# Other places for the mask preparation in the emission order of a two-layer graph network kernel

## Chip, cores and metric

The kernel runs on one core of one Trainium2 chip. The metric is the device time of one execution in microseconds (us); the median of three runs of the kernel before is 3479.84 us (3477.9 to 3487.6).

## The reference

Sixteen graphs of 1024 nodes with 256 features each go through two layers, each added to its input. `adj` is an int32 matrix of 1024 x 1024 zeros and ones per graph.

```python
h = relu(layernorm(x))                              # layer 0: masked attention + MLP
n = layer_norm(h, gamma1, beta1)                    # query = key = value = n, 8 heads of 32
scores = einsum('bhqd,bhkd->bhqk', n, n) / sqrt(32)
attn = softmax(where(adj[:, None] > 0, scores, -inf))
h = h + einsum('bhqk,bhkd->bhqd', attn, n)
x = x + h + gelu(layer_norm(h, gamma2, beta2) @ W1 + b1) @ W2 + b2
f = relu(layernorm(x))                              # layer 1: graph attention
g = f @ W
e = leaky_relu(g @ a_1 + (g @ a_2).T + (g @ a_12) @ g.T, 0.2)
p = softmax(where(adj > 0, e, -9e15))
x = x + elu(f @ W_1 + (p @ f) @ W_2)
```

Both layers use the same adjacency.

## The kernel before, in words

All work on one graph is a batch `b`. The attention of layer 0 for batch `b` (`attention`, L954) is done at the same time as the MLP and layer 1 of batch `b - 1` (`rest`, L1099), so that TensorE always has something to do.

**Units and groups.** The attention of a batch is cut into 32 units (qh, g, kt): half of the queries (512), group of four heads, tile of 128 keys. A unit scores its keys against its queries (L975, 16 small matmuls into two PSUM tiles `s`), adds the mask (L996, VectorE, two instructions of 128 x 1024) and takes the exponential (L999, ScalarE) into an SBUF tile `e`. In the next unit TensorE multiplies `e` with the values (L1012). A group is the eight units with the same half and the same heads; it ends after units 8, 16, 24 and 32. The sums of the exponentials over the keys are made by DMA: GpSimd issues for each `e` an accumulating DMA into the group's first tile (L1036, 512 KB each). The pool of `e` has five buffers; a buffer comes free when its accumulating DMA has landed. Two to three units after the end of a group TensorE adds up the accumulated tiles over the partitions (`den`, L914), which waits for the last accumulations.

In batch 0 there is no `rest` beside the attention. There half of the mask additions are done by TensorE, with a matmul of the mask and an identity (L968), and half of the sums by VectorE (L1023).

**Masks.** For each half of the queries, four tiles of 128 rows of the adjacency are prepared (`turn_masks`, L875):

- `fetch_mask` (L579): two DMAs of 256 KB each (128 x 512 int32) on SP's queue, L583. The pool has two such buffers, so a tile can be fetched only once the one before it is converted.
- `convert_mask` (L587): two VectorE instructions (L591) turn 0 and 1 into a large negative number and 0 in fp8, tile `mq` (two buffers).
- a transposing DMA on SP's queue (L887) puts the tile into `mk`, the mask of that half of the queries with the keys on partitions.

The generator makes one step at a time: step 0 fetches tile 0; step 1 converts tile 0 and fetches tile 1; step 2 transposes tile 0, converts tile 1 and fetches tile 2; step 3 and 4 go on in the same way; step 5 transposes tile 3. A mask `mk` lives for two batches, since layer 1 of the same graph reads it one batch later (L1266). The pool `mkp` has four: those of two batches. Step 2 is the first to write into the buffer of the same half of two batches before. The first half of batch 0 is prepared in `prologue` (L822 to L854) and isn't touched by the change.

**Order.** Every engine works its instructions in the order in which they are emitted, kept by L1495 to L1504. The order is made by streams, generators that say at which place they want to go on (L1474 to L1479): the stream with the smallest place makes its next step. Places are counted in batches. `stream_a` puts attention unit k of batch b at place b + k/32. `stream_b` puts the pieces of `rest` beside them, by their estimated TensorE time against 134 us per batch. `stream_c` puts the loading and normalizing of the next batch (`prologue`, L760) at b - 0.70 to b - 0.25. `stream_m` (L1461) puts the steps of the masks; `spread` (L1409) divides the stretch from start to end into five, and step i is made at start + i/5 of it. Small deferred pieces are inserted by an estimated clock (`defer`, L743).

Of the kernel before, what the change touches and what calls it, by code (L numbers as in the profile page):

```python
# [493 lines left out]
def fast_path(  # L494
# [84 lines left out]
    def fetch_mask(b, t):  # L579
        halves = []  # L580
        for c in range(0, N, QW):
            a = adjp.tile([P, QW], I32, tag="adj", name=f"adj_{b}_{t}_{c}")
            nc.sync.dma_start(a, rows(adj, b, t, slice(c, c + QW)))  # L583
            halves.append(a)
        return b, t, halves

    def convert_mask(b, t, halves):  # L587

        m = mqp.tile([P, N], FP8, tag="mq", name=f"mq_{b}_{t}")
        for i, a in enumerate(halves):  # L590
            nc.vector.tensor_scalar(  # L591
                m[:, i * QW : (i + 1) * QW], a, 0.0, NEG8, op0=ALU.is_le, op1=ALU.mult, saturate=False
            )
        return m
# [280 lines left out]
    def turn_masks(b, qh, st):  # L875

        ts = list(range(qh * TPH, (qh + 1) * TPH))
        raw = fetch_mask(b, ts[0])
        yield
        m = mkp.tile([P, NT // 2, QW, 2], FP8, tag="mk", name=f"mk_{b}_{qh}")  # L880
        st[qh] = m
        pairs = m.rearrange("p m q r -> p m (q r)").bitcast(BF16)
        mq = convert_mask(*raw)
        raw = fetch_mask(b, ts[1])
        for i in range(TPH):
            yield
            nc.sync.dma_start_transpose(pairs[:, :, i * P : (i + 1) * P], mq.bitcast(BF16))  # L887
            if i + 1 < TPH:
                mq = convert_mask(*raw)
            if i + 2 < TPH:  # L890
                raw = fetch_mask(b, ts[i + 2])
# [517 lines left out]
    def spread(pieces, n, start, end):  # L1409
        yield start  # L1410
        for i, _ in enumerate(pieces):
            yield start + (end - start) * (i + 1) / n

    states = [{} for _ in range(B + 1)]
# [46 lines left out]
    def stream_m():  # L1461
        for b in range(B):
            for qh in range(b == 0, NQH):
                yield from spread(turn_masks(b, qh, states[b]), 5, b + 0.5 * qh - 0.27, b + 0.5 * qh - 0.07)

    def stream_s():
        yield -0.3
# [3 lines left out]
        for i, _ in enumerate(check_products()):  # L1471
            yield 1.32 + 0.04 * i

    streams = [stream_s(), stream_a(), stream_b(), stream_p(), stream_c(), stream_m()]  # L1474
    places = [next(s, None) for s in streams]
    while any(p is not None for p in places):
# [93 lines left out]
```

## Time and profile before

| | |
|---|---|
| median of 3 runs | 3479.84 us |
| all runs | 3477.9, 3479.84, 3487.6 us |
| the profiled execution, its time | 3473.44 us |
| the profiled execution, its span | 3471.6 us, mean granted TensorE clock 0.997 |
| VectorE waits for an adjacency fetch (L591), whole span | 14.0 us in 14 waits, longest 4.1 us |
| PE waits for the mask addition (L975 for L996), whole span | 3.1 us in 2 waits |
| adjacency fetch, from issue to landing | min 3.0, median 5.6, max 10.6 us |
| transposing DMA, from issue to landing | median 6.2 us |
| conversion (L591), one instruction | median 0.42 us |
| DMA engines, share of the span by queue | GpSimd's (accumulations) 71.3%, SP's 15.5% |

How to read it: a stretch of the trace is given as from:to in us from the start of the span. "Busy" is the time in which an engine executes; the DMA share is the mean busy share of the core's 16 DMA engines, and goes over 1 where times of packets overlap. An arrow in brackets behind a line tells how long the engine was idle before it, and what ended that. The first attention unit starts at 25.6 us; those of batch 0 take 126 us in all, those of batch 1 207 us, later ones 211 to 212 us. In batch 4, unit 0 starts at 782.6 us.

### The profile page before, as it was taken

The numbers are of one execution on the slowest core, as the hardware profiler recorded it, in microseconds if no ns is written. First come the engines' busy times: TensorE is split into PE (matmuls) and PEld (weight loads), VectorE is DVE, ScalarE is ACT, GpSimd is POOL, SyncE is SP. The second block draws the span as 40 slices with busy tenths as digits, with TensorE's granted clock in tenths as the row PEclk, the third lists the DMA queues.
The fourth block names the chain that finished last, engine by engine and source line by source line (L and its number), as shares of the span: only waits on it lengthen the run. The fifth ranks groups of instructions, "written<-read, shape, count | busy, mean of one in ns | idle before, by whom it ended". The sixth has DMA issues, their size and how long they took to land.

```text
span 3471.6 us, 119040 instructions
## 1 busy us (share of the span) xinstructions
PE 3424.4 (99%) x52478; PEld 1648.9 (47%) x52478; DVE 2749.4 (79%) x5194; ACT 1857.3 (53%) x2184; POOL 1418.5 (41%) x1708
## 2 busy tenths in 40 slices
PE   6999999999999999999999999999999999999998
PEld 2244444444444444444444444444444444444477
DVE  6788788787888878888788887878888788887754
ACT  5555555555555555555555555555555555555522
POOL 4443443434434344443444434344343444434220
PEclk9999999999999999999999999999999999999999
DMA  8798989899899998989999899998999989899720
GB/s 193 147 186 171 187 163 191 177 188 192 161 190 177 187 192 165 185 171 190 189 167 188 170 187 182 183 188 167 189 177 193 187 164 185 166 192 182 152 62 14
DMA packets 281906, 598.56 MB, mean 172 GB/s; under 512 B 94882, under 2 KB 130084, under 8 KB 281380
## 3 DMA queue, kind: packets, MB, share of 16 engines
q0 software_dynamic: 124416, 453.04, 71.3%
q1 hardware_dynamic: 156676, 137.56, 15.5%
q8 instruction: 414, 6.78, 0.8%
q14 instruction: 112, 0.92, 0.1%
q10 hardware_dynamic: 288, 0.26, 0.0%
HBM read 104.21 MB, written 16.78 MB: 35 GB/s over the span
## 4 chain that ended last, share of the span: by engine, by line
PE 95%; DMA 2%; DVE 1%; issue 1%; ACT 1%; POOL 0%; SPq 0%; POOLq 0%; DVEq 0%; ACTq 0%
PE s L975 15%; PE o L1012 14%; PE pa L570 12%; PE ph L570 12%; PE lg L570 12%; PE po L570 11%; PE pf L570 3%; PE pg L570 3%; PE puT L570 3%; PE den L914 2%; DMA acc<-e 2%; PE pty L1142 1%; PE ptos L946 1%; PE ptk L808 1%; PE ptf L1218 1%; PE pa L567 1%
## 5 line engine op out<-in xcount | busy, mean ns | idle before, releaser
L999 ACT ACTIVATE e<-e 128x1024 f32<-128x1024 f32 x852 | 895.9, 1057 | 947.0 <-DVE e L996 703.3
L1036 POOL DMA_DIRECT2D acc<-e x864 | 757.3, 892 | 1444.9 <-DMA acc<-e 657.8
L996 DVE TENSOR_TENSOR e<-s,mk 128x1024 f32<-128x1024 f32 x852 | 1003.2, 1217 | 185.4 <-PE s L975 151.4
L975 PE MATMUL s<-kT 32*64 32x512 f32 x8192 | 578.3, 616 | 3.1 <-DVE odd L996 3.1
L1012 PE MATMUL o<-e,va 128*32 128x512 f32 x3456 | 463.8, 606 | 2.1 <-ACT e L999 2.1
L570 PE MATMUL pa<-gw,e 128*32 128x258 f32 x7648 | 455.2, 380 | 0.0
L570 PE MATMUL lg<-fT,uT 128*32 128x256 f32 x7680 | 449.3, 379 | 0.0
L570 PE MATMUL ph<-yT,w 128*32 128x256 f32 x7808 | 447.8, 379 | 0.0
L570 PE MATMUL po<-w,hid 128*32 128x256 f32 x7680 | 439.8, 379 | 0.0
L570 PEld LDWEIGHTS ph<-yT,w 128*32 128x32 f32 x7808 | 259.4, 110 | 197.8 <-issue 42.5
L570 PEld LDWEIGHTS po<-w,hid 128*32 128x32 f32 x7680 | 249.9, 110 | 209.4 <-issue 62.2
L570 PEld LDWEIGHTS lg<-fT,uT 128*32 128x32 f32 x7680 | 259.1, 110 | 189.3 <-issue 38.5
L570 PEld LDWEIGHTS pa<-gw,e 128*32 128x32 f32 x7648 | 253.4, 110 | 198.7 <-issue 48.8
L1272 ACT ACTIVATE e<-e,shift 128x512 f32<-128x512 f32 x256 | 183.1, 717 | 187.2 <-DVE e L1271 167.0
L1266 DVE SCALAR_TENSOR_TENSOR e<-lg,gw,mk 128x256 f32<-128x256 f32 x512 | 223.0, 477 | 71.1 <-PE lg L570 60.7
L1169 DVE TENSOR_TENSOR hid<-ph,b1c 128x512 f32<-128x512 f32 x256 | 175.2, 687 | 86.0 <-PE ph L570 74.6
L1012 PEld LDWEIGHTS o<-e,va 128*32 128x32 f32 x3456 | 69.0, 108 | 354.9 <-issue 226.6
L1271 DVE SCALAR_TENSOR_TENSOR e<-e 128x512 f32<-128x512 f32 x256 | 196.2, 766 | 8.8
L999 ACT ACTIVATE acc<-acc 128x1024 f32<-128x1024 f32 x124 | 130.9, 1057 | 130.2 <-DVE acc L996 125.8
L975 PEld LDWEIGHTS s<-kT 32*64 32x64 f32 x8192 | 121.1, 130 | 163.8 <-issue 108.4
L996 DVE TENSOR_TENSOR acc<-s,mk 128x1024 f32<-128x1024 f32 x124 | 146.0, 1217 | 20.6 <-PE s L975 20.5
L800 POOL TENSOR_TENSOR nrm<-nrm,g 128x256 f32<-128x256 f32 x128 | 113.1, 884 | 61.7 <-DVE nrm L734 61.7
(146 smaller groups left out, 3820.1 us busy)
## 6 DMA issues: line engine op xcount, KB each, us to landing
acc<-e POOLq DMA_DIRECT2D x864, 512.0 KB, 6.2
adj<-in_adj_dram SPq DMA_DIRECT2D x248, 256.0 KB, 5.5
h<-in_x_dram SPq DMA_DIRECT2D x64, 256.0 KB, 6.0
xb<-in_x_dram SPq DMA_DIRECT2D x128, 128.0 KB, 4.6
out_dram<-z SPq DMA_DIRECT2D x128, 128.0 KB, 3.7
adj<-in_adj_dram SPq DMA_DIRECT2D x4, 512.0 KB, 6.9
mk<-mq SPq DMA_TRANSPOSE x128, 6.2
w<-in_L_gnn_W_dram SPq DMA_DIRECT2D x2, 1024.0 KB
```

Source lines behind the costliest of these rows:

```text
L570: nc.tensor.matmul(out[c : c + HD], lhsT[:, c : c + HD], rhs, start=start, stop=stop)
L800: nc.gpsimd.tensor_mul(nrm, nrm, g1)
L914: nc.tensor.matmul(den[j * HD : (j + 1) * HD, :], ones, acc[j // 2][:, j % 2, :], start=acc is accs[0], stop=acc is accs[-1],)
L975: nc.tensor.matmul(sc[j // 2][c : c + P // 2, j % 2, :], kT[r, g, kt * P + c : kt * P + c + P // 2], kT[r, g, qs], start=j >= by_pe, stop= ...
L996: nc.vector.tensor_tensor(e, masked, mb, op=ALU.add)
L999: weights = lambda e=e, masked=masked: nc.scalar.activation(e, masked, AF.Exp, scale=SCALE)
L1012: nc.tensor.matmul(o[j * HD : (j + 1) * HD, :], va[:, kt, (g * GH + j) * HD : (g * GH + j + 1) * HD], es[j // 2][:, j % 2, :], start=(kt = ...
L1036: nc.gpsimd.dma_start(sums[g, qh][i], e, accum_op=ALU.add)
L1169: nc.vector.tensor_tensor(hid[:, f0 : f0 + 2, :], ph, b1c[:, f0 : f0 + 2].unsqueeze(2).to_broadcast([P, 2, CW]), op=ALU.add,)
L1266: nc.vector.scalar_tensor_tensor(e[:, j, :], lg[:, j, :], gw[:, kt, D : D + 1], st[c // 2][:, kt // 2, qs, kt % 2], op0=ALU.add, op1=ALU.add,)
L1271: nc.vector.scalar_tensor_tensor(e, e, ALPHA, e, op0=ALU.mult, op1=ALU.max)
L1272: ready = defer(2.5, lambda: nc.scalar.activation(e, e, AF.Exp, bias=shift))
```

## The change

One line: the places between which the five steps of a mask are spread. Stretches in batches, b being the batch that the mask is for.

```diff
     def stream_m():
         for b in range(B):
             for qh in range(b == 0, NQH):
-                yield from spread(turn_masks(b, qh, states[b]), 5, b + 0.5 * qh - 0.27, b + 0.5 * qh - 0.07)
+                yield from spread(turn_masks(b, qh, states[b]), 5, b + (-0.34, 0.05)[qh], b + (-0.10, 0.40)[qh])
```

| in units of the batch in which it is made | start, end before | distance of steps | start, end after | distance of steps |
|---|---|---|---|---|
| first half (made in the batch before) | 23.4, 29.8 | 1.28 | 21.1, 28.8 | 1.54 |
| second half (made in the same batch) | 7.4, 13.8 | 1.28 | 1.6, 12.8 | 2.24 |

The second half is first read in unit 16, the first half in unit 0 of its batch. The number and kind of instructions on every engine and queue stay as they are.

## The prediction, made blind

> **What bounds the kernel now.** I read the page's busy table and its chain first, then the chain in order of time, then the busy time by stretches of one batch, then the start-up. From the page:
>
> ```profile
> PE 3424.4 (99%) x52478; PEld 1648.9 (47%) x52478; DVE 2749.4 (79%) x5194; ACT 1857.3 (53%) x2184; POOL 1418.5 (41%) x1708
> ...
> PE   6999999999999999999999999999999999999998
> ...
> PE 95%; DMA 2%; DVE 1%; issue 1%; ACT 1%; POOL 0%; SPq 0%; POOLq 0%; DVEq 0%; ACTq 0%
> ```
>
> TensorE has work from the second fortieth of the span to the last and carries 95% of the chain. Busy time alone doesn't say that there is no stall inside it, so I look at the rhythm. The chain in order of time shows the same stage (the logits matmuls, L570) once per batch:
>
> ```profile
> 540.59 3.52 PE lg L570 x64
> ...
> 752.51 3.52 PE lg L570 x64
> ...
> 963.36 3.52 PE lg L570 x64
> ...
> 1174.19 3.52 PE lg L570 x64
> ...
> 3074.81 3.52 PE lg L570 x64
> ```
>
> The distances are 211.92, 210.85 and 210.83 us. The shortest returns in many batches, so I take 210.84 us as the period without a stall. From the first to the last of these lines are 12 batches in 2534.22 us, or 211.19 each: over 12 batches all stalls together are 12 x 0.35 = 4.2 us, over the 14 steady batches 4.9 us. No change of places alone can win more there.
>
> Busy time by stretches of batch 4 (units 0 to 4, 4 to 9, 9 to 14, 14 to 21, 21 to 25, 25 to 30, 30 to 32; columns: length, busy us of PE, PEld, DVE, ACT, POOL, clock, DMA share, GB/s):
>
> ```profile
> 782.60:809.10 26.50, 26.50 (x432) 12.05 (x432) 19.14 (x30) 15.77 (x17) 11.11 (x14) 1.00 0.78 156
> 809.10:843.70 34.60, 34.60 (x566) 16.79 (x560) 26.98 (x50) 19.25 (x16) 15.55 (x20) 1.00 0.95 189
> 843.70:877.90 34.20, 34.20 (x571) 16.86 (x567) 27.92 (x63) 19.19 (x22) 15.06 (x19) 1.00 1.05 218
> 877.90:922.00 44.10, 44.10 (x656) 19.73 (x656) 34.47 (x69) 24.00 (x35) 22.61 (x28) 1.00 0.76 143
> 922.00:950.60 28.60, 28.60 (x456) 13.34 (x444) 25.63 (x43) 15.55 (x22) 11.46 (x14) 1.00 0.88 175
> 950.60:979.90 29.30, 29.30 (x504) 14.52 (x496) 25.38 (x54) 14.52 (x19) 9.72 (x11) 1.00 1.10 210
> 979.90:993.50 13.60, 13.60 (x225) 6.45 (x217) 12.89 (x24) 7.67 (x10) 5.32 (x6) 1.00 1.02 208
> ```
>
> The two stretches in which masks are made now (843.7 and 950.6) have the fullest DMA, 1.05 and 1.10; the others have 0.76 to 1.02. VectorE is fullest at the end (12.89 of 13.60). PE is full in all of them: the crowding costs it nothing in this batch.
>
> In the start-up there are real gaps:
>
> ```profile
> 60.00:80.00 20.00, 18.06 (x292) 6.80 (x285) 14.80 (x35) 11.61 (x19) 6.07 (x8) 0.99 0.95 203
> 80.00:100.00 20.00, 17.78 (x184) 4.37 (x183) 17.09 (x34) 12.97 (x17) 13.17 (x16) 0.84 0.59 117
> ...
> 120.00:140.00 20.00, 17.48 (x192) 4.90 (x186) 10.47 (x18) 8.64 (x9) 3.79 (x4) 0.91 0.78 161
> 140.00:160.00 20.00, 18.12 (x230) 6.70 (x232) 18.69 (x27) 7.23 (x7) 7.21 (x9) 0.91 0.96 213
> ```
>
> and in order of time, two of them begin with a mask conversion that waits for its adjacency:
>
> ```profile
> 74.59 0.90 DVE L591 TENSOR_SCALAR mq<-adj 128x512 fp8e5<-128x512 int32 x2 [0.98 <-DMA adj<-in_adj_dram]
> ...
> 77.95 1.09 PE L975 MATMUL s<-kT 32*64 32x512 f32 x8 [1.27 <-DVE odd L996]
> ...
> 140.01 0.43 DVE L591 TENSOR_SCALAR mq<-adj 128x512 fp8e5<-128x512 int32 x1 [1.15 <-DMA adj<-in_adj_dram]
> ...
> 142.91 1.09 PE L975 MATMUL s<-kT 32*64 32x512 f32 x8 [1.88 <-DVE odd L996]
> ```
>
> VectorE waits 0.98 and 1.15 us, the masked addition behind it (L996) is late, and PE waits 1.27 and 1.88 us for it. A third (4.12 us at 127) coincides with a wait of PE for the last accumulating DMA (2.35 us). After the first and the third the granted clock of the stretch drops: 20 x 0.16 = 3.2 us and twice 20 x 0.09 = 1.8 us, 6.8 us in all.
>
> **What the skill says.** "Perfetto Trace Analysis", section "Identifying the Most-Contended Engine": matmul busy time is no good measure of the distance from the limit. That is why I use the period; the trace agrees in so far as batches with 99 to 100% busy time differ by 1.1 us. "DMA: Bandwidth & Descriptors", section "Issuing engines are not separate DMA queues": DMAs of all issuing engines run on the same 16 engines and interleave. The shares above 1 where masks and accumulations meet agree. "TensorE: Matmul & The Clock Gate", section "Part 1": the array falls to half clock after an idle window of about 3.4 us. Here the clock fell after gaps of 1.3 to 2.4 us, shorter than that, so I count the clock as something that may or may not be lost with each gap.
>
> **The change, part by part.** Nothing is added or removed: the same 124 mask tiles (31 half-batches of four), each of two fetches of 256 KB, two conversions and one transposing DMA, are put elsewhere. With 32 attention units per batch, the old places of the four transposes are units 9.9, 11.2, 12.5, 13.8 (second half) and 25.9, 27.2, 28.5, 29.8 (first half of the next batch); the new ones 6.1, 8.3, 10.6, 12.8 and 24.2, 25.7, 27.3, 28.8. The distance from a fetch to its conversion grows from 1.28 units to 2.24 and 1.54.
>
> 1. *Conversions on VectorE.* Two of 0.42 us per tile, in order with everything else. The built order shows them ahead of L996 of units 4, 7, 9 and 11 (before: 9, 10, 12, 13) and 23, 25, 26 and 28 (before: 25, 26, 28, 29). Behind a moved conversion wait L996, ScalarE's exponential and then PE. By the instructions in order of time (end of L996, start of the next unit's L975; smallest of batches 3 to 14), L996 ends 3.7, 3.5, 1.7 and 2.8 us ahead of the next unit's scores in units 4, 7, 9, 11, and 4.1, 2.0, 2.6 and 0.5 in 23, 25, 26, 28. The last carries a conversion already, so 0.84 us is covered everywhere; without that cover it would cost up to 0.84 us a batch. Unit 29, also with 0.5 us to spare, loses its conversion. Some of the small steady stalls lie there: I take 1 us over all batches, bounds 0 and 2.4.
>
> 2. *Fetches and transposes on the DMA engines.* SP's hardware queue moved 137.56 MB in 15.5% of 3471.6 us, 3.9 us per MB of all engines' time: 2.0 us for a tile's fetch; for its transpose of 0.13 MB in small packets at least 0.5, and I take 0.8. Counted by the new places, units 9 to 14 (843.7) lose two fetches and a transpose, 4.8 us of 34.2: 1.05 to 0.91. Units 0 to 4 gain two fetches, 4.0 of 26.5: 0.78 to 0.93. Units 4 to 9 gain a transpose: 0.95 to 0.97. Units 25 to 30 give one fetch to units 21 to 25: 1.10 to 1.03, and 0.88 to 0.95. The crests fall. What a crest cost: accumulations late, their e buffers late, L996 waiting, 6.9 us in eight waits from 220 to 3300 us, of which PE sees at most the 4.9 us. I take 1.5 us saved, bounds -2.5 and +14 (rival B).
>
> 3. *SP's queue.* The first transpose writes the buffer that the masks of two batches ago held; its last reader is now just ahead. In the built order the output store ahead of it on SP waits for a later VectorE instruction than that reader, so the wait is covered and costs nothing. Behind it on SP stand the next fetches, wanted 1.5 units (some 10 us) later against 5.6 us to landing: covered too. Loads of x (L770) are passed by one or two fetches; nobody waits for them at once. POOL's queue holds no step of the change; its accumulations only share the engines.
>
> 4. *Start-up.* Units of batch 0 last some 2.8 to 4 us, so 1.28 units are 4 to 5 us, less than the 5.6 us median to landing: hence the waits. 2.24 units are about 6.5 us, 1.54 about 4.5. The second half of batch 0 should lose its wait (1.27 us of PE, and the clock's 3.2 if it follows the gap); batch 1's first half stays short of the landing. The first tile comes behind the weights on SP's queue, whose transfers ended near 39 us; its conversion is due near 40 us: no stall, at most 1 us. Saved: between -2 and 12 us; I take 2.5.
>
> **Sum.** 1 + 1.5 + 2.5 = 5 us. The profiled execution took 3473.44 us (span 3471.6 and 1.8 around it): 3468.4 after. The median of the runs is 6.4 us above it, 3479.84: forecast 3475.
>
> **Rivals.** (A) *Nothing moves*: PE is the bound and only other covered work shifts. For it: PE is full in all seven stretches; against: the start-up gaps. 3480 to 3484. (B) *Slower*: short crests. In units 6 and 8 a fetch and a transpose now start together, 2.8 us of DMA work in some 6 us whose share was 0.91 to 0.98 already. Accumulations finish up to 2.8 us later, an e buffer comes late, L996 waits, and beyond the 2.0 us that it has to spare in unit 6 PE stops. With accumulations late by their usual jitter too (longest wait for one 1.7 us) I price it at 1.0 us in each of 14 batches: +14 us, 3494; it is slower beyond the bound from 0.75 us per batch. For it: only 5 e buffers. Against: averages of 1.05 and 1.10 over five units are borne now. (C) *Everything comes back*: 4.9 steady, the two waits of 1.27 and 1.88, and 6.8 of clock, less a little: about -15 us, 3465.
>
> **Numbers.** Forecast 0.52 (3470 to 3480), A 0.18, B 0.14, C 0.16. A measurement of this kernel tells about 0.3% (10.4 us) from no change: faster 0.16, same 0.70, slower 0.14. The range 3462 to 3489 leaves out B and the far third of C, 0.19.
>
> **What would show it.** Right: period 210.84 with fewer longer batches; no wait of L591 near 60 and 75 us; DMA share near 0.91 in units 9 to 14; PE still 99%. Wrong: a period that exceeds 210.84 in every batch, waits of L996 for accumulations in units 4 to 9, or a new wait of L591 near 40 us.

## The result and the profile after

The changed kernel takes 3535.1 us (median of 4 runs, 3522.24 to 3545.12); the kernel before, in runs beside it, 3483.72 us (4 runs, 3477.9 to 3496.59). The ratio is 1.0150, 95% interval 1.0127 to 1.0173: slower by some 51 us. That is far above the range. The profiled execution of the changed kernel took 3545.12 us (span 3543.3, mean clock 0.994), the slowest of the four; its span is 71.7 us longer than that of before.

The page after, in the parts that the prediction read first:

```profile
PE 3451.1 (97%) x52478; PEld 1669.8 (47%) x52478; DVE 2757.9 (78%) x5194; ACT 1857.6 (52%) x2184; POOL 1415.8 (40%) x1708
...
PE 82%; DMA 11%; DVE 4%; issue 2%; ACT 1%; POOL 0%; SPq 0%; POOLq 0%; DVEq 0%; ACTq 0%
```

PE has fallen from 99% to 97%, and DMA from 2% to 11% of the chain: transfers now release the work that ends last. Which ones, the two lists of waits say (line waited for: us in total, times, longest). PE's first:

```profile
PE den L914 <- DMA acc<-e: 38.9, 14, 7.1
```

and VectorE's:

```profile
DVE mq L591 <- DMA adj<-in_adj_dram: 38.0, 33, 3.8
...
DVE e L996 <- DMA acc<-e: 8.8, 6, 2.2
```

The same two lines in the kernel before:

```profile
PE den L914 <- DMA acc<-e: 2.3, 1, 2.3
...
DVE mq L591 <- DMA adj<-in_adj_dram: 14.0, 14, 4.1
```

So there are two new waits, and neither is the one that the prediction feared: L996 waiting for an `e` buffer stands at 8.8 us, of 6.9 before.

Where in a batch they lie shows when the start of every attention unit (first L975 matmul of a unit) is listed and the shortest length of each unit over batches 2 to 14 is subtracted. The shortest lengths add up to 210.81 us per batch in both kernels. In batches 2 to 15 of the changed kernel unit 10 is too long by 49.6 us in all (0 to 10.8 a batch; before 1.0), units 26 to 30 by 14.1 us (before 3.2). Batch 1 is 11.4 us longer than before. These are 48.6 + 10.9 + 11.4 = 70.9 of the 71.7 us. The start-up saved nothing: batch 0 lasts 125.8 us in both.

Not all of the 49.6 us is standing still. `den` waits 29.3 us of it; and behind the waits of four batches the granted clock is at half for 3 to 6 us of work, 18.1 us in all, so that some 9 us are lost there (an estimate from the clock records). Behind the wait of batch 6, for instance (the 0.50 is the clock):

```profile
1304.60:1311.40 6.80, 4.36 (x40) 1.82 (x44) 0.00 (x0) 1.54 (x2) 0.00 (x0) 0.50 0.93 208
```

The rest of the 49.6 us was not followed.

**Unit 10.** The chain in order of time, changed kernel, batch 6, the end of the first group:

```profile
1277.54 7.77 DMA acc<-e
...
1285.84 6.12 DMA acc<-e
...
1292.50 14.49 DMA acc<-e
1306.99 0.04 issue
1307.04 0.65 PE den L914
```

and the timeline of the same stretch:

```profile
1279.63 4.21 SPq L887 DMA_TRANSPOSE mk<-mq  x1
...
1285.84 0.85 POOL L1036 DMA_DIRECT2D acc<-e  x1 [4.08 <-DMA acc<-e]
...
1291.33 2.61 SPq L887 DMA_TRANSPOSE mk<-mq  x1
...
1292.50 0.85 POOL L1036 DMA_DIRECT2D acc<-e  x1 [1.62 <-DMA acc<-e]
...
1293.99 5.76 SPq L770 DMA_DIRECT2D h<-in_x_dram  x2
...
1307.04 1.07 PE L914 MATMUL den<-acc,ones 128*32 128x512 f32 x2 [6.98 <-DMA acc<-e]
```

An accumulating DMA adds into the tile that an earlier one wrote, so its issue on POOL waits for that one to land (the 4.08 us in brackets). A group has two tiles and so two such chains; the three accumulations above are of one. One that is stretched by a transpose beside it puts all later ones of its chain back. The last one, issued 0.9 us after unit 9 began, meets a transpose, two loads of x and the first two accumulations of the next group, and takes 14.5 us; PE stands still for 6.98 us. In the same batch before, the last one was issued 1.0 us ahead of unit 9 and landed 1.0 us after unit 10 began:

```profile
1261.51 0.85 POOL L1036 DMA_DIRECT2D acc<-e  x1 [1.61 <-ACT acc L999]
```

Over batches 2 to 14 the last accumulation of the first group landed on average 0.9 us ahead of the start of unit 10 before, at the latest 2.8 us after it; the matmuls of `den` that read it begin 2.4 us after that start when nothing holds them up. In the changed kernel it landed 4.6 us after it on average, at the latest 10.0. The last accumulations of the second and third group hardly differ (within 0.6 us on average).

The places are not yet the times of issue: SP issued the transposes ahead of them. By the traces (median of batches 2 to 14) the second half's four are issued at 5.0, 7.2, 9.1 and 11.0 units in the changed kernel, at 9.2, 10.4, 12.0 and 12.7 before. `den` begins near 10.2. So three are ahead of it where there was one, and the new ones are those at 5.0 and 7.2.

**Unit 26.** The timeline of the changed kernel, batch 4, units 25 to 27:

```profile
964.90 0.75 DVE L591 TENSOR_SCALAR mq<-adj 128x512 fp8e5<-128x512 int32 x2
965.02 0.34 SPq L1318 DMA_DIRECT2D out_dram<-z  x1
...
965.41 2.03 SPq L887 DMA_TRANSPOSE mk<-mq  x1
...
967.54 1.00 SPq L583 DMA_DIRECT2D adj<-in_adj_dram  x2
...
973.77 0.43 DVE L591 TENSOR_SCALAR mq<-adj 128x512 fp8e5<-128x512 int32 x1 [2.44 <-DMA adj<-in_adj_dram]
...
975.43 0.43 DVE L591 TENSOR_SCALAR mq<-adj 128x512 fp8e5<-128x512 int32 x1 [1.24 <-DMA adj<-in_adj_dram]
...
976.79 3.69 PE L570 MATMUL pa<-gw,e 128*32 128x258 f32 x64 [0.98 <-DVE e L1266]
...
977.29 2.35 DVE L996 TENSOR_TENSOR e<-s,mk 128x1024 f32<-128x1024 f32 x2
```

The tile is converted at 964.90, its buffers come free, but the next fetch stands on SP behind an output store and the transpose of the tile before, and is issued at 967.54. Its conversion comes one unit later and waits 2.44 and 1.24 us. The work behind it on VectorE (L1266 of layer 1, then L996) is late, and PE with it. The conversions in units 25 and 26 waited 29.8 us in batches 2 to 14, of 0.9 before.

**What the prediction had named as signs.** Busy time by stretches of batch 4, changed kernel, same units as before:

```profile
800.10:826.60 26.50, 26.50 (x432) 12.03 (x432) 18.19 (x30) 15.79 (x17) 9.81 (x14) 1.00 0.81 167
826.60:861.20 34.60, 34.60 (x564) 16.83 (x560) 28.24 (x52) 19.29 (x16) 16.11 (x20) 1.00 1.02 207
861.20:896.20 35.00, 35.00 (x572) 17.98 (x565) 28.15 (x59) 19.34 (x22) 15.91 (x20) 1.00 0.95 194
```

The crest in units 9 to 14 fell as said, from 1.05 to 0.95 (0.91 forecast), and units 4 to 9 rose from 0.95 to 1.02 (0.97 forecast); units 0 to 4 stand at 0.81 (0.93 forecast). The shares look harmless, with no stretch above the crest of before; yet it is in the third of these stretches that the stalls of most batches lie.

### The profile page after: what moved, and what is told of

It reads as the page before. It is cut to its first block, busy times and chain, and to the rows that moved or that the text cites. A ratio compares the mean times of both kernels' runs of the same rounds, so it can differ in the third digit from the quotient of the medians.

```text
span 3543.3 us, 119080 instructions
## 1 busy us (share of the span) xinstructions
PE 3451.1 (97%) x52478; PEld 1669.8 (47%) x52478; DVE 2757.9 (78%) x5194; ACT 1857.6 (52%) x2184; POOL 1415.8 (40%) x1708
## 4 chain that ended last, share of the span: by engine, by line
PE 82%; DMA 11%; DVE 4%; issue 2%; ACT 1%; POOL 0%; SPq 0%; POOLq 0%; DVEq 0%; ACTq 0%
PE s L975 13%; PE pa L570 11%; PE o L1012 11%; PE lg L570 11%; DMA acc<-e 9%; PE po L570 9%; PE ph L570 8%; PE pg L570 3%; PE puT L570 3%; PE pf L570 3%; PE den L914 1%; DMA adj<-in_adj_dram 1%; DVE e L996 1%; PE ptf L1218 1%; PE ptk L808 1%
## 5 line engine op out<-in xcount | busy, mean ns | idle before, releaser
L996 DVE TENSOR_TENSOR e<-s,mk 128x1024 f32<-128x1024 f32 x852 | 1003.2, 1217 | 201.1 <-PE s L975 140.7
L975 PE MATMUL s<-kT 32*64 32x512 f32 x8192 | 582.5, 614 | 1.5 <-DVE e L996 1.5
L570 PE MATMUL ph<-yT,w 128*32 128x256 f32 x7808 | 459.4, 380 | 0.0
L570 PE MATMUL po<-w,hid 128*32 128x256 f32 x7680 | 457.3, 383 | 0.0
L570 PEld LDWEIGHTS lg<-fT,uT 128*32 128x32 f32 x7680 | 261.7, 110 | 186.9 <-issue 38.9
L1266 DVE SCALAR_TENSOR_TENSOR e<-lg,gw,mk 128x256 f32<-128x256 f32 x512 | 222.9, 476 | 53.9 <-PE lg L570 43.8
L975 PEld LDWEIGHTS s<-kT 32*64 32x64 f32 x8192 | 122.4, 130 | 164.6 <-issue 97.9
L996 DVE TENSOR_TENSOR acc<-s,mk 128x1024 f32<-128x1024 f32 x124 | 146.1, 1218 | 20.6 <-PE s L975 20.4
L1196 DVE TENSOR_TENSOR xb<-po,xb 128x256 f32<-128x256 f32 x128 | 54.3, 424 | 130.6 <-PE po L570 115.4
```

The source lines that it names most:

```text
L570: nc.tensor.matmul(out[c : c + HD], lhsT[:, c : c + HD], rhs, start=start, stop=stop)
L975: nc.tensor.matmul(sc[j // 2][c : c + P // 2, j % 2, :], kT[r, g, kt * P + c : kt * P + c + P // 2], kT[r, g, qs], start=j >= by_pe, stop= ...
L996: nc.vector.tensor_tensor(e, masked, mb, op=ALU.add)
L1196: nc.vector.tensor_add(xt[t], po, xt[t])
L1266: nc.vector.scalar_tensor_tensor(e[:, j, :], lg[:, j, :], gw[:, kt, D : D + 1], st[c // 2][:, kt // 2, qs, kt % 2], op0=ALU.add, op1=ALU.add,)
```

## The experiments

All ratios are to the kernel before, run beside them on the same chip. The diffs are shortened, and shown against the changed kernel; those of experiments 9 and 10 against the kernel before.

**1 and 2. Each half alone.**

```diff
-  b + (-0.34, 0.05)[qh], b + (-0.10, 0.40)[qh]
+  b + (-0.34, 0.23)[qh], b + (-0.10, 0.43)[qh]      # first half only
+  b + (-0.27, 0.05)[qh], b + (-0.07, 0.40)[qh]      # second half only
```

> Only the first half of the queries has the new places (start -0.34, end -0.10); the second half has the old ones. Theory (accumulations of the group that ends after unit 8 land late because mask DMAs run beside them in units 4 to 10, and TensorE waits for them at den, L914): the long stall at unit 10 goes, the small one at unit 26 stays (about 10 us over the run in the trace of after), so 3485 to 3497. Rival (VectorE: conversions and their waits for adjacency delay L996, in both halves alike): about half of the 52 us remain, near 3510.

Measured: 3494.11 us, ratio 1.0049 (1.0029 to 1.0069). `den` waits 3.0 us in one wait, L591 42.8 us in 36: as expected.

> Only the second half of the queries has the new places (start 0.05, end 0.40). Theory: nearly the whole loss, 3520 to 3535, with PE waiting for the accumulating DMA at den in unit 10. Rival (both halves alike by VectorE's order): near 3510.

Measured: 3533.53 us, ratio 1.0153 (1.0132 to 1.0175), as expected. L591 waits 12.9 us in 6 waits, and of PE's waits:

```profile
PE den L914 <- DMA acc<-e: 45.8, 19, 8.8
```

So each wait belongs to one half: `den` to the second, the adjacency near unit 26 to the first. The two losses (17 and 53 us) add up to more than the 51 us of both together; why, these runs don't tell.

**3. `den` one unit later.** If the wait for the last accumulation is the loss, more time before it should remove it. The finished groups of the first four heads, of both halves of the queries, are held back by one unit on their way to `total`:

```diff
+        was_held = held[:]
...
-        summed.extend(was_weighed)
+        for args in was_weighed:
+            (held if args[2] == 0 else summed).append(args)
+        summed.extend(was_held)
```

> The changed kernel, with the sums of groups 0 and 2 (den, L914) taken one unit (6 to 8 us) later, all DMAs and conversions where the change puts them. Theory: den is the only victim, the longest wait of 10.8 us shrinks to 3, most vanish: 3485 to 3500. Rival (late e buffers or VectorE's order stop the scores of the same units, den only shows it): the time stays at 3525 to 3540, and the stall moves to L975 or L1012.

Measured: 3508.57 us (3490.85 to 3515.6), ratio 1.0096 (1.0078 to 1.0115): faster than the changed kernel, but not the 3485 to 3500 us that were expected. The waits of `den` are gone from the trace, whose execution is the fastest of this kernel's runs. But the shortest period is 211.36 us, 0.55 more per batch, and PE waits 14.7 us in 14 waits for a reciprocal (L937) that now comes at a worse place. This supports the cause, with a cost of its own mixed in.

**4. Fetches and conversions early, transposes later.** The second half keeps its new places for fetching and converting (four `mq` buffers instead of two); its four transposes go to places 11.4, 12.2, 13.0 and 13.8.

```diff
-    mqp = pool("mqp", 2)
+    mqp = pool("mqp", 4)
...
+        for i in range(TPH):
+            mqs.append(convert_mask(*raw))
+            if i + 1 < TPH:
+                raw = fetch_mask(b, ts[i + 1])
+            yield
+        for i in range(TPH):
+            nc.sync.dma_start_transpose(pairs[:, :, i * P : (i + 1) * P], mqs[i].bitcast(BF16))
+            yield
```

> The changed kernel, with the second half's fetches and conversions at the new places, but its four transposing DMAs moved behind den, to units 11.4 to 13.8 (four mq buffers). If the transposing DMAs ahead of den (at 6.1, 8.3 and, in the trace, 9.1) are what delays the accumulations: stall at unit 10 gone, 3485 to 3500. If the fetches (0.5 MB each at 3.8, 6.1, 8.3) are: 3520 to 3535. If it is the sum of both: in between.

Measured: 3494.58 us, ratio 1.0057 (1.0037 to 1.0076), as expected. `den` waits 7.9 us in 5 waits, of 38.9 in 14:

```profile
PE den L931 <- DMA acc<-e: 7.9, 5, 3.0
```

What is left is about what the first half costs alone (1.0049). But not all four transposes came behind `den`: SP issued them at 9.2, 10.3, 10.7 and 11.0 units. One is still ahead of `den`, as in the kernel before; what the experiment took away are those at 5.0 and 7.2.

**5. The first half's last two conversions later.** Second half at the old places; the first half as changed but for steps 3 and 4, so that tile 2 is converted two units after its fetch.

```diff
-  spread(turn_masks(b, 0, ...), 5, b - 0.34, b - 0.10)     # 21.1 22.7 24.2 25.7 27.3 28.8
+  for at in (21.12, 22.66, 24.19, 26.4, 27.9, 28.8)
```

> First half as in the changed kernel but for its last two conversions: steps 3 and 4 at 26.4 and 27.9 of the batch before instead of 25.7 and 27.3, so that tile 2 is converted two units after its fetch and not one. Second half at the old places. Theory (a conversion only one unit after its fetch waits for the adjacency, the mask addition of unit 26 behind it is late): the waits of L591 near unit 26, 27 us over batches 2 to 14, go to under 10 us, and the time falls from 1.005 to 1.000 to 1.002 of the kernel before, 3479 to 3487 us. Rival (the place of the first half as a whole costs, its transposes among the accumulations of the last group): time stays at 1.004 to 1.006, about 3494 us, while the waits of L591 go.

Measured: 3482.34 us (13 runs), ratio 1.0008 (0.9999 to 1.0018), as expected. L591 waits 11.2 us in all, of 42.8 with the evenly spread steps, and the transposes of the first half are still among the accumulations of the last group. So the loss went with the waits, as the theory of the one unit between fetch and conversion has it. The two steps also hold two transposes and a fetch, which moved with the conversions by some 0.6 units; that these matter was not tried by itself.

**6. First half old, second half as in experiment 4.**

> First half at the old places; second half with fetches and conversions at the new, early places and its four transposes behind den, 11.4 to 13.8. Theory (of the second half only the transposes ahead of den cost anything, the fetches and conversions nothing): 0.999 to 1.001 of the kernel before, 3476 to 3483 us. If fetches or conversions in units 1.6 to 10.6 cost something too: 1.002 or more, over 3486 us. If early fetches gain something that the late ones had lost, under 3474 us.

Measured: 3485.58 us (14 runs), ratio 1.0015 (1.0007 to 1.0023), between the two expectations. Early fetches and conversions, with the transposes at 9.2 to 11.0 units instead of 9.2 to 12.7, cost some 5 us, not nothing: the last accumulation lands 2.3 us after the start of unit 10 on average, at the latest 4.3, and `den` waits 7.2 us in 6 waits. They use up the slack; they don't go far beyond it.

**7. Two of the four transposes early.** As experiment 4, but the first two transposes at places 6.1 and 8.3, the last two at 12.2 and 13.0. In the trace they are issued at 5.0, 7.3, 10.3 and 11.0: the two new ones are there, and none near 9.1.

> As the kernel with the second half's four transposes late, but the first two of them at their new places, 6.1 and 8.3, the last two at 12.2 and 13.0; fetches, conversions and the first half as in the changed kernel. That kernel stands at 3494.6, the changed one at 3533 to 3535. Theory that only the third transpose, at 10.6 by its place and about 9.2 by the trace, together with the loads of x, meets the group's last accumulation: like the one with all four late, 3491 to 3499 us. Rival that every transpose ahead of den puts the chain of accumulations back by some us: two of three remain, some 26 of the 39 us, 3516 to 3526 us.

Measured: 3513.35 us, ratio 1.0092 (1.0072 to 1.0111); `den` waits 26.2 us in 16 waits. Both expectations missed. Against experiment 4 the first two of the three cost 18.8 of some 40 us by the medians, 12 of 32 by the ratios: it is not the third alone, but whether each costs alike the intervals leave open. The landings tell the same: 3.9 us after the start of unit 10 on average, between 2.3 (experiment 4) and 4.6 (all early).

**8. Loads of x later.** The changed kernel, with the stream that loads and normalizes the next batch 1.9 units later.

```diff
-  spread(prologue(b, states[b]), 28, b - 0.700, b - 0.250)
+  spread(prologue(b, states[b]), 28, b - 0.640, b - 0.190)
```

> The changed kernel, but the stream that loads and normalizes the next batch 0.06 batches (1.9 units) later, so that its loads of x come behind den of the first group of heads. Theory that the loads of x share in the collision (they begin at 9.1 units, with the third transpose): the waits of den for its last accumulation fall from 38.9 to under 20 us and the time to 3510 to 3522 us. Rival that the transposes alone do it: den's waits stay over 30 us, the time at 3530 to 3540 us. Something else may be moved with it: then the time rises while den's waits fall.

Measured: 3560.38 us, ratio 1.0237 (1.0221 to 1.0253). PE's waits:

```profile
PE ptk L808 <- DVE e L1266: 42.8, 14, 3.7
...
PE den L914 <- DMA acc<-e: 16.8, 13, 3.9
```

`den`'s waits fell from 38.9 to 16.8 us while the time rose: a step that was moved along (L808) brings a wait of its own in each of 14 batches, and the shortest period is 213.51 us. In its trace the first two loads of x are still issued ahead of `den`, at 9.3 and 9.6 units instead of 9.0 and 9.5. So it is not shown whether the loads of x share in the collision. They can't be the cause alone: the kernel before issues the first of them at 9.1 units too, without harm.

**9 and 10. The suspect by itself.** The kernel before with its masks where they were, and three more DMAs per batch on SP's queue at the places of the three early transposes. They write to a tile that nobody reads: once as transposes, once as plain loads of the same 128 KB.

```diff
+    def stream_x():
+        for b in range(1, B):
+            for at in (6.08, 8.32, 10.56):
+                yield b + at / 32
+                nc.sync.dma_start_transpose(extra, extra_in)                      # 9
+                nc.sync.dma_start(extra, rows(adj, b, 0, slice(0, QW // 2)))      # 10
```

> The kernel before, with three more transposing DMAs in each of batches 1 to 15, from a tile of zeros to a tile that nobody reads, 128 KB each, on SP's queue at 6.1, 8.3 and 10.6 units; the masks stay at their old places. Theory (transposes ahead of den lengthen the accumulations and push den back, whatever else is moved): den waits for its last accumulation in most batches, 20 to 45 us in all, and the time is 3510 to 3535 us, of 3478 for the kernel before. Rival (not the transposes but the new order of fetches and conversions, or SP's queue before the loads of x): 3478 to 3488 us.

> The kernel before, with three more plain loads in each of batches 1 to 15, 128 KB each (128 x 256 int32 of the adjacency) to a tile that nobody reads, on SP's queue at the same places as the three extra transposes. Theory that it is the kind of transfer (small packets) and not its bytes: den's waits under 8 us, time 3478 to 3488 us. Rival that any 128 KB there delay the accumulations: like the extra transposes, within 10 us of them.

Measured: the transposes 3509.43 us, ratio 1.0086 (1.0058 to 1.0114); the loads 3481.39 us, ratio 0.9999 (0.9986 to 1.0011). The loads did as expected; the transposes cost just less than the 3510 to 3535 us expected, and `den` waited 12.9 us, not the 20 to 45 us expected. One reason is in the traces: the three are issued at 4.9, 5.9 and 10.3 units (the loads at 4.9, 5.7 and 10.2), so that two and not three are clearly ahead of `den`. The waits with the transposes, PE's and then VectorE's:

```profile
PE den L917 <- DMA acc<-e: 12.9, 6, 4.9
```

```profile
DVE e L999 <- DMA acc<-e: 52.3, 42, 3.5
```

and PE's with the loads:

```profile
PE den L915 <- DMA acc<-e: 4.3, 3, 2.1
```

It is the kind of transfer and not its bytes. The rows of SP's queue (packets, MB, share of 16 engines' span), before, with the transposes and with the loads:

```profile
q1 hardware_dynamic: 156676, 137.56, 15.5%
```

```profile
q1 hardware_dynamic: 181156, 143.46, 17.5%
```

```profile
q1 hardware_dynamic: 163156, 143.46, 16.4%
```

The 45 transposes bring 76 us more, in 544 packets each, the loads 32 us, in 144 packets each. Not all of that is their own. The packet records of the traces, sorted by size, tell it apart (each sum divided by 16 engines). The transposes' own packets of 256 B take 40 us, 0.88 each; the loads' own of 1024 B take 18 us, 0.40 each. Packets of 2048 B, those of the mask fetches and of loads of x, are as many as before, and take 18 us more beside the transposes, 4 us more beside the loads. The rest are packets of 4 B that come with each transfer. The accumulations' packets, on GpSimd's queue, take 36 us more with the transposes and 9 us less with the loads.

The same records show the harm directly. In batches 2 to 14 of the kernel before, a packet of 4096 B of an accumulation took 345 ns on average when it began with none of SP's data packets under way, 355 ns beside those of 2048 B, 351 ns beside those of 1024 B, but 504 ns beside a transpose's, and 741 ns with a transpose and packets of 2048 B together. In the changed kernel these are 346, 351, 353, 545 and 722 ns.

Part of the 28 us of experiment 9 is the `e` buffer wait that rival B described, 52.3 us on VectorE of 6.9 before; in its trace unit 10 is too long by 19 us, units 13 to 16, behind the third transpose, by 12 us.

**11. Both repairs in the changed kernel.** Experiment 4's second half with experiment 5's first half.

> The changed kernel with both repairs at once: the second half's four transposes behind den (11.4 to 13.8), its fetches and conversions at the new places, and the first half's last two conversions at 26.4 and 27.9. If the two causes account for the whole loss and what is left of each part adds up (1.0008 and 1.0015 when tried alone), the ratio is 1.0023, about 3488 us; between 1.001 and 1.0035 counts as that. Over 1.005: a cause of the loss is still missing, which only the two halves together bring. Under 1.000: the longer stretches do win something once both collisions are gone.

Measured: 3480.21 us (14 runs), ratio 1.0004 (0.9991 to 1.0017), a little under the 1.001 to 1.0035 expected. The loss is accounted for: with one transpose ahead of `den` instead of three (9.2 units in the trace) and two units between the third fetch and its conversion, new and old places can't be told apart. No version beat the kernel before; its stalls leave 4.9 us to win over the steady batches, about the half width of this interval (4.5 us).

## Why the prediction was wrong, step by step

- *What bounds the kernel*: right. The period without stalls is 210.81 us in both kernels; all loss comes on top of it.
- *Step 2, fetches and transposes*: this step failed, in three places. First the victim. It followed late accumulations to the `e` buffers and L996 ("of which PE sees at most the 4.9 us"), though the description of the kernel says that `den` waits for the last of them. In the steady batches of before `den` hardly waited, and that was read as no danger; its slack, 3.3 us on average (0.9 us ahead of unit 10 and 2.4 to the matmuls that read it) and none in the worst batch, was never measured. Second the term for a transpose, "at least 0.5, and I take 0.8". As the share of its own packets that was right: in the kernel before they take 108 us for 128 tiles, 0.85 each. What it put at nothing is what a transpose does to the packets beside it: an accumulation's took 504 to 545 ns there instead of 345, and 45 transposes cost 28 us where 45 loads of the same bytes cost none (experiments 9 and 10). Third the way to count: average shares of stretches of five units can't show a chain of DMAs in which each waits for the one before. Its upper bound, 14 us, was therefore too low by a factor of more than three: 48.6 us in unit 10 of the traced execution. The count itself was off by one as well: by their places two transposes, not one, come into units 4 to 9, and two, not one, leave units 9 to 14. One of the two fetches that it gave to units 0 to 4 is issued at 4.1 in the trace.
- *Step 1, "0.84 us is covered everywhere"*: the conversions' own time was covered, as the changed kernel with both repairs shows. The wait that they bring along was not: a conversion that waits in VectorE's order for its adjacency delays what is behind it: by 2.44 and 1.24 us in the trace above, 3.7 together, more than the 2.6 us that the step gave unit 26 to spare.
- *Step 3, "wanted 1.5 units (some 10 us) later ... covered too"*: failed. The mean distance is 1.5 units, but the built order in step 1 already put two conversions ahead of L996 of units 25 and 26, one unit apart, and the fetch between them is issued behind a store and a transpose. In the trace above VectorE was free for the conversion 3.8 us after the fetch was issued (967.54 to 971.33), with 6.0 us to a median landing. Steps 1 and 3 cost 17 us (experiment 1), and nearly all of it went when the two steps with these conversions were put later within the same stretch (experiment 5).
- *Step 4, the start-up*: the gains came and were taken back in the same batch. In batch 0 of the changed kernel no conversion waits for its adjacency near 60 and 75 us for more than 0.3 us, and near 41 us one waits 0.71, as allowed; but `den` of the first group waits for its accumulation, the same wait as later:

```profile
66.34 0.63 PE L914 MATMUL den<-acc,ones 128*32 128x512 f32 x2 [2.60 <-DMA acc<-e]
```

  Unit 10 of batch 0 lasts 9.05 us, of 4.23 before. This takes back 4.8 of the 7.3 us that units 14, 15 and 30 gained (6.56 to 4.25, 4.53 to 2.77, 7.45 to 4.27); units 16 and 17 take back another 2.7 us, whose cause was not followed.
- *Rivals*: B had the side, the cause (a fetch and a transpose starting together make accumulations late) and nearly the place, units 6 and 8; it had the wrong thing waiting, and a price of 1.0 us per batch where 3.5 (48.6 / 14) was measured. Its argument against itself, that averages of 1.05 and 1.10 are borne now, compared stretches that begin at about a `den` with one that leads up to it.

## What to carry to other kernels

Before a transfer is moved, list what has to land at the end of the stretch that it moves into, and measure that deadline's slack in every repetition, the worst one first: a chain of dependent DMAs with 3 us to spare showed in no list of waits here, and passed on every delay. Price a move by what the transfer does to its neighbours, not by its bytes. And where steps are spread evenly, check the distances in the built order, which come in whole units: here an average of 1.5 was a 1 where it mattered.

## What the runs showed of the hardware

Beside the accumulations, the packets of a transposing DMA of 128 KB from SBUF to SBUF took 2.2 times the DMA engines' time of those of a plain load of 128 KB from DRAM (0.88 against 0.40 us). The Trainium skill, "Advanced Engine Details and Errata", section "X-Bar Transpose (TRN2)", has transposing DMAs as fast as regular ones on this chip; in this traffic that is not what was measured.

More important is what they do to others: an accumulation's packet took 504 ns beside a transpose and 355 beside mask fetches and loads of x, against 345 alone, and 45 transposes cost 28 us where 45 loads cost none. The stretched packets are on GpSimd's queue and so not behind SP's. Whether the small packets or the transposing path stretch them, and whether the time for which SP is held (2.5 us median for issuing one of the extra transposes) adds to the loss, the runs don't separate.

Second, the harm is uneven: with the same instructions in each batch, unit 10 of the changed kernel was too long by 0 to 10.8 us. The profiled mean clock fell from 0.997 to 0.994, some 11 us of the 3543.3 us span. Four of its stretches at half clock begin within a wait of `den` in unit 10; whether the clock fell only because of the stalls was not tried by itself.
